# Pair 0's low halves between the unpackings of the weight words, its first products tile by tile, and five small operations moved from VectorE to GpSimd

## The chip, the cores and the metric

The kernel runs on one core of a Trainium2 chip. The metric is the device time of one execution in microseconds. Five engines work at the same time, each on its own queue of instructions in a fixed order: TensorE (PE; its weight loads are shown apart as PEld), VectorE (DVE), ScalarE (ACT), GpSimd (POOL), and SyncE (SP), which only issues transfers here. An instruction that must wait for another engine holds up everything behind it on its own queue.

## The reference, cut to what matters

```python
W  = cond_weights[condition]                    # (64, 64, 64): one of 16 matrices for each batch
h  = einsum('bct,bcd->bdt', x, W)               # x: (64, 64, 1024) f32
p  = qweight.reshape(N, groups, 3)              # words that hold 6-bit fields
v0, v1, v2, v3 = p[..,0] & 63, p[..,0] >> 6 & 63, p[..,1] & 63, p[..,2] & 63
w  = (unpacked - zero_point) * scale            # (1024, 1024)
out = x + einsum('bsk,nk->bsn', h, w) + bias
```

So there are two products in a row. The first mixes the 64 channels of a batch by a matrix that the batch's condition selects; the second multiplies each of the 64 x 64 rows by a 1024 x 1024 weight matrix that has to be unpacked from words.

## The kernel before, in words

**Tiling.** The 64 batches go as 32 pairs; a pair fills the 128 partitions with 2 x 64 channels. For each pair, stage 1 makes `ph`, the first product, turned so that the features of the sequence lie on the partitions in 8 tiles of 128 (`kt` 0 to 7). It is split into two float16 halves: `hh`, the rounded value (ScalarE), and `hl`, the rest (VectorE). Stage 2 multiplies both by the unpacked words `q16`, read as float16 numbers, and sums 8 tiles x 2 halves x 2 banks of 512 columns into `po`: 32 matmuls of 512 columns a pair. The zero point, scale, bias and residual come after it, in `zero_points`, `scale_out`, `accumulate` and their early forms.

**Order.** The schedule is by hand (`manual_schedule`): each engine executes its instructions in the order in which the Python code calls the helpers. From pair 3 on, `window(p)` repeats one pattern; pairs 0 to 2 have an opening written out call by call (lines 573 to 713), and the whole change lies there.

**The opening.** Pairs 0 and 1 (group 0) use a float32 first product on the raw selected matrices, since the split table isn't there yet: `early_stage1` (L436), `early_high` (L444, ScalarE, one pass for each half of 64 columns), `early_low` (L451, VectorE, likewise one pass for each half). Pair 0's `ph` lies in two tiles, `ph0a` for `kt` 0 to 3 and `ph0b` for 4 to 7. `unpack` (L153 and L155, VectorE) turns the words into `q16`: tiles 0 and 1 singly as their words land, then 2-3, 4-5 and 6-7. `stage2_tiles` (L520) issues the products of some tiles of a pair; with `[0]` the `hh` part alone, with `[1]` the `hl` part. `weights_turn` puts a 128-column matmul `pt` (L174) into TensorE's queue, the first step towards the powers of two that scale the 16 matrices.

**The table of matrices.** `weights_scaled` (GpSimd, L196) scales them, `weights_high` (ScalarE, L201) and `weights_low` (VectorE, L204) split them into the table `tab`. `select_pair` (L249) then copies two entries of `tab` for each pair; for pairs 2 to 7 GpSimd does it, 12 copies, with one large product, `zsc`, after the first two. The numbers of the entries are loaded into GpSimd's registers by `conditions_of` (L235), early in its queue. Stage 1 of pair 2 needs the first two copies. Behind the copies GpSimd makes the low half of pair 2's and 3's sums (`sums_low`, L354), which the matmuls `pu` of `feature_sums` (L365) read.

**Group 1 (pairs 2 and 3)** is split on the whole: `magnitudes` (L273, ScalarE) sums the absolute values, `bounds` (L277, a matmul `pl`) adds them over the partitions, `scales` (L138, L139, L142, VectorE) makes powers of two, `stacked_high` (L322, ScalarE) and `stacked_low` (L330, VectorE, both inputs in SBUF) write the halves of x into `xa`. `FIRST` is pair 2, `SECOND` pair 3.

**The end of pairs 0 and 1.** `early_zero_points` (L464, ScalarE), `early_minus` (L469) and `early_res` (L475, both VectorE); `early_minus` needs the factor `u` that `early_unscales` (L432, two operations of 64 partitions x 1 element a pair) makes. `weights_hot` (L208) makes a one-hot table of the conditions that `weights_of_batches` (L224) needs much later.

Of the kernel before, what the change touches and what calls it, by code (L numbers as in the profile page):

```python
# [14 lines left out]
ALU = mybir.AluOpType  # L15
# [4 lines left out]
QUNIT = 2.0**-24  # L20
# [9 lines left out]
def adaln_ffn(ctx: ExitStack, tc: tile.TileContext, x, cond, cw, qw, ws, wz, bias, out):  # L30
    nc = tc.nc
    B, C, T = x.shape
    _, _, NK, _ = cw.shape
# [6 lines left out]
    LO, HI = slice(0, C), slice(C, P)  # L40
# [10 lines left out]
    unpacking = ExitStack()  # L51
# [31 lines left out]
    cb = const.tile([NK, B], I32, name="cb")  # L83
# [44 lines left out]
    kio = const.tile([NK, 1], F32, name="kio")  # L128
# [6 lines left out]
    def powers(sums, up, down, least=True):  # L135

        if least:
            nc.vector.tensor_scalar(sums, sums, LEAST, None, ALU.max)  # L138
        nc.vector.tensor_scalar(  # L139
            down.bitcast(I32), sums.bitcast(I32), EXPONENT, EXPONENT, ALU.bitwise_and, ALU.bitwise_xor  # L140
        )
        nc.vector.tensor_scalar(up.bitcast(I32), sums.bitcast(I32), EXPONENT, None, ALU.bitwise_and)  # L142
# [5 lines left out]
    def unpack(kt, n=1):  # L148

        w = kt if kt < 2 else kt - 2 if kt < 6 else kt - 4  # L150
        to, of_ = q16[:, kt : kt + n, :], qr[:, w : w + n, :]
        if kt in (2, 3, 6, 7):
            nc.vector.tensor_scalar(to, of_, 6 if kt < 4 else 8, 63, ALU.logical_shift_right, ALU.bitwise_and)  # L153
        else:
            nc.vector.tensor_scalar(to, of_, 63, None, ALU.bitwise_and)  # L155
# [9 lines left out]
    hot = const.tile([P, B], BF, name="hot")  # L165
# [23 lines left out]
    def weights_powers():  # L189

        powers(tmp["pw"], tmp["pw"], wdn)
# [8 lines left out]
    def weights_high():  # L200
        nc.scalar.copy(tab[:, :, 0, :], wsc)  # L201
# [3 lines left out]

    def weights_hot():

        nc.vector.tensor_scalar(hot[0:NK, :], cb, kio[:, 0:1], None, ALU.is_equal)  # L208

    def weights_own():  # L210

# [44 lines left out]
    st = {}  # L256
    BOTH = slice(0, 2)

    def magnitudes(g, i):
        if g not in st:  # L260
            st[g] = {
                "l1": sp.tile([P, 2], BF, name="l1"),
                "u": sp.tile([P, 2], F32, name="u"),
                "hs": sp.tile([P, 2], F32, name="hs"),
                "xs": sp.tile([P, 2], F32, name="xs"),
                "up": sp.tile([P, 2], F32, name="up"),
                "down": sp.tile([P, 2], F32, name="down"),
                "hf": ap.tile([P, 2, T], F16, name="hf"),
                "lf": ap.tile([P, 2, T], F16, name="lf"),
                "xa": ap.tile([P, 2, 2, T], F16, name="xa"),  # L270
            }
        junk = ap.tile([P, T], BF, name="junk", bufs=1)
        nc.scalar.activation(junk, xts[g][:, i, :], AF.Abs, accum_out=st[g]["l1"][:, i : i + 1])  # L273

    def bounds(g, sl=BOTH):
        pl = ps_s.tile([P, 2], F32, name="pl", tag="s")
        nc.tensor.matmul(pl[:, sl], lhsT=ones, rhs=st[g]["l1"][:, sl], start=True, stop=True)  # L277
        st[g]["pl"] = pl

    def scales(g, sl=BOTH):  # L280
        powers(st[g]["pl"][:, sl], st[g]["up"][:, sl], st[g]["down"][:, sl])
# [23 lines left out]
    def split_2(g, i, ts_=ALL):  # L305

        nc.vector.scalar_tensor_tensor(  # L307
            st[g]["lf"][:, i, ts_],
            xts[g][:, i, ts_],
            st[g]["down"][:, i : i + 1],  # L310
            st[g]["hf"][:, i, ts_],
            ALU.mult,
            ALU.subtract,
        )
# [11 lines left out]
    def stacked_low(g, i, j):  # L326

        h, o = HALVES_OF[j]
        xa = st[g]["xa"]
        nc.vector.scalar_tensor_tensor(  # L330
            xa[o, i, j], xts[g][h, i], st[g]["down"][h, i : i + 1], xa[h, i, j], ALU.mult, ALU.subtract
        )
# [7 lines left out]
    def stack_low(g, sl=BOTH, ts_=ALL):  # L340
        lf, xa = st[g]["lf"], st[g]["xa"]
        nc.sync.dma_start(xa[HI, sl, 0, ts_], lf[LO, sl, ts_])
        nc.sync.dma_start(xa[LO, sl, 1, ts_], lf[HI, sl, ts_])
# [41 lines left out]
    updown = const.tile([P, 2, 2, 2], F32, name="updown")  # L385

    def early_select(p, j, eng):

        h = (LO, HI)[j]
        k = eng.value_load(cb[0:1, 2 * p + j : 2 * p + j + 1], min_val=0, max_val=NK - 1)  # L390
        for n, o in enumerate((LO, HI)):
            to = wbd[h, p, j * D + n * D // 2 : j * D + (n + 1) * D // 2]
            of_ = wq[o, ds(k, 1), :].rearrange("p o d -> p (o d)")
            if eng is nc.scalar:
                eng.copy(to, of_)
            else:
                eng.tensor_copy(to, of_)

    def early_weights(p):

        wl = const.tile([P, 1], F32, name=f"wl{p}")
        nc.vector.tensor_reduce(wl, wbd[:, p, :], AX.X, ALU.max, apply_absolute_value=True)
        nc.vector.tensor_scalar(wm[:, p, :], half, wl[:, 0:1], None, ALU.mult)
# [23 lines left out]
    def early_scales(p):  # L427
        powers(tmp["pl"], updown[:, p, 0, :], updown[:, p, 1, :], least=False)

    def early_unscales(p):  # L430
        for j, h in enumerate((LO, HI)):
            nc.vector.tensor_scalar(st[0]["u"][h, p : p + 1], updown[h, p, 0, j : j + 1], 0.5 / QUNIT, None, ALU.mult)  # L432

    def early_stage1(p, ph, kts=range(KT)):
        for kt in kts:
            nc.tensor.matmul(  # L436
                ph[:, kt % ph.shape[1], :, :], lhsT=xts[0][:, p, ts(kt, P)], rhs=wbd[:, p, :], start=True, stop=True
            )
# [6 lines left out]
                hs_pair[p][0][:, kts, h], ph[:, :, j, :], AF.Copy, scale=updown[:, p, 1, j : j + 1]  # L445
            )

    def early_low(p, ph, kts):
        hh, hl = hs_pair[p]
        for j, h in enumerate((LO, HI)):  # L450
            nc.vector.scalar_tensor_tensor(  # L451
                hl[:, kts, h], ph[:, :, j, :], updown[:, p, 1, j : j + 1], hh[:, kts, h], ALU.mult, ALU.subtract
            )
# [19 lines left out]
    def early_res(p):  # L473
        tmp["res", p] = late.tile([P, N], F32, name=f"res{p}")
        nc.vector.tensor_tensor(tmp["res", p], pos[p], scb, ALU.mult)  # L475
# [34 lines left out]
    def stage1_low(p, ph, kts=slice(0, KT)):  # L510
        hh, hl = hs_pair[p]
        nc.vector.tensor_tensor(hl[:, kts, :], ph[:, kts, :], hh[:, kts, :], ALU.subtract)  # L512
# [17 lines left out]
    def stage2_tiles(p, kts, ks=range(2)):  # L530
        if p not in pos:
            pos[p] = ps_o[1 + p % 2].tile([P, N], F32, name="po", tag="po")
        products(pos[p], p, kts, ks, BANKS, BANKS)
# [40 lines left out]
    FIRST, SECOND = slice(0, 1), slice(1, 2)  # L574
    LOWER, UPPER = slice(0, KT // 2), slice(KT // 2, KT)
# [7 lines left out]
    ph0a, ph0b = [ps_e.tile([P, KT // 2, 2, D], F32, name="ph0") for _ in range(2)]  # L583
# [2 lines left out]
    early_select(0, 1, nc.scalar)  # L586
    early_select(1, 0, nc.gpsimd)
    early_select(1, 1, nc.gpsimd)
    for n in range(2, 8):
        conditions_of(n, nc.gpsimd)  # L590
    weights_largest()
# [8 lines left out]
    early_stage1(0, ph0b, range(4, KT))  # L600
    early_bounds(0, 3)
    early_scales(0)
    early_weights(1)
    early_high(0, ph0a, LOWER)
    early_high(0, ph0b, UPPER)
    early_stage1(1, ph1)
    unpack(0)
    unpack(1)
    early_low(0, ph0a, LOWER)
    early_magnitudes(1, 0, ALL, nc.scalar)  # L610
    stage2_tiles(0, range(0, 2), [0])
    unpack(2, 2)
    early_low(0, ph0b, UPPER)
    early_rows(1, 0)
    weights_turn()
    weights_diagonal()
    weights_hot()
    unpack(4, 2)
    stage2_tiles(0, range(0, 2), [1])
    unpack(6, 2)  # L620
    early_sums(0)
    early_sums(1)
# [1 line left out]
    weights_bounds()  # L624
    early_bounds(1, 1)
    early_scales(1)
    weights_powers()
    weights_scaled()
    weights_own()
# [8 lines left out]
    stacked_high(1, 0)  # L638
    for j in range(2):
        stacked_low(1, 0, j)  # L640
    weights_high()
    stage2_tiles(0, range(6, KT))
    early_feature_sums(0)
    early_feature_sums(1)
    magnitudes(1, 1)
    early_zero_points(0)
    early_unscales(0)
    weights_up()
    weights_low()
    unpacking.close()  # L650
    late = ctx.enter_context(tc.tile_pool(name="late", bufs=1))
    select_pair(2, nc.gpsimd)
    nc.gpsimd.tensor_tensor(zsc, zsb, scb, ALU.mult)
    for n in range(3, 8):
        select_pair(n, nc.gpsimd)


    stage2_tiles(1, range(0, 4), [0])
    stage2_tiles(1, range(0, 4), [1])
    bounds(1, SECOND)  # L660
    scales(1, SECOND)
    early_minus(0)
    early_res(0)
    stage2_tiles(1, range(4, 7))
    stacked_high(1, 1)
    stacked_low(1, 1, 0)
    ph = stage1(2)
    stage1_high(2, ph, LOWER)
    stage1_high(2, ph, UPPER)
# [2 lines left out]
    magnitudes(2, 0)  # L672
    magnitudes(2, 1)
    stage1_low(2, ph)
    stacked_low(1, 1, 1)
    weights_of_batches()
    unscales(1)
    early_unscales(1)


    sums_high(1)
# [4 lines left out]
    ph = stage1(3)  # L686
# [7 lines left out]
    split_1(2, 0)  # L694
    stack_high(2, FIRST)
    split_2(2, 0)
    stack_low(2, FIRST)
    split_1(2, 1)
    stack_high(2, SECOND)
    stage1_low(3, ph)  # L700
    stage2_bank(2, 0, [1])
    stage2_bank(2, 1, [1])
    split_2(2, 1)
# [81 lines left out]
    p = NP - 1  # L785
# [81 lines left out]
```

## Time and profile before

| what | value |
| --- | --- |
| time, median of 3 runs | 266.2 us (266.08 to 266.25) |
| the profiled execution: its own time | 266.35 us |
| the profiled execution: span of its instructions | 264.6 us |
| TensorE busy | 260.1 us, 98% of the span |
| VectorE busy | 202.1 us, 76% |
| ScalarE busy | 162.0 us, 61% |
| GpSimd busy | 175.8 us, 66% |
| granted TensorE clock, mean | 0.999 |

The time of an execution holds 1.75 us more than the span, which begins with the first instruction of the program and ends with its last. Lines of the profile that list instructions give the start in us from the start of the span, the duration in us, the engine, the line of the code, the operation, the tile written and the tiles read (`out<-in`), the shapes, how many instructions are merged, and in brackets how long the engine sat idle before it and what ended that. A merged line hides a long instruction among short ones, so short windows are asked for where single instructions matter. A record of an instruction ends a little after the next one on its engine may start.

### The profile page before, as it was taken

What the parts mean: (1) busy time and instruction counts of PE and PEld (TensorE: products, weight loads), DVE (VectorE), ACT (ScalarE), POOL (GpSimd) and SP (SyncE); (2) the same over time, 40 slices, a digit from 0 to 9 for tenths busy, and PEclk for the clock granted to TensorE, in tenths of its full rate; (3) what the DMA queues carried; (4) which work ended last, traced back from release to release, by engine and by line L of the source; (5) the groups of instructions that cost most, each with busy time, mean ns of one, the idle gap of its engine ahead of it and who ended that gap; (6) DMA issues with size and microseconds to landing.
All of it is one profiled execution on the core that took longest, in us unless ns stands there. A gap on an engine that the chain in (4) does not pass through costs nothing.

```text
span 264.6 us, 5769 instructions
## 1 busy us (share of the span) xinstructions
PE 260.1 (98%) x2175; PEld 140.2 (53%) x2175; DVE 202.1 (76%) x272; ACT 162.0 (61%) x290; POOL 175.8 (66%) x106
## 2 busy tenths in 40 slices
PE   8999999999999999999999999999999999999995
PEld 8645555555455555455555445555545555545544
DVE  4889999695967949498695968949497695955535
ACT  4899899655766556686555667556586555634100
POOL 5037367879595996959689595986929286495200
PEclk9999999999999999999999999999999999999999
DMA  6993087759639786579867797676976664551104
GB/s 207 388 408 153 5 190 245 215 177 290 192 103 310 212 286 171 186 229 242 258 185 226 245 260 243 155 246 209 288 221 188 199 180 144 165 161 79 81 7 154
DMA packets 32300, 53.60 MB, mean 203 GB/s; under 512 B 15120, under 2 KB 15504, under 8 KB 32272
## 3 DMA queue, kind: packets, MB, share of 16 engines
q1 hardware_dynamic: 32240, 53.23, 65.0%
q8 instruction: 17, 0.28, 0.4%
q14 instruction: 11, 0.09, 0.1%
q10 hardware_dynamic: 32, 0.00, 0.0%
HBM read 20.19 MB, written 16.78 MB: 140 GB/s over the span
## 4 chain that ended last, share of the span: by engine, by line
PE 95%; DMA 2%; SPq 1%; DVE 1%; issue 0%
PE po L520 81%; PE ph L496 11%; PE pe L520 3%; DMA qr<-in_L_ffn_qweight_dram 2%; SPq L66 1%; PE pu L365 1%; DVE hl L451 0%; SPq L78 0%; SPq L89 0%; DVE pe L561 0%; PE pu L458 0%; DVE xt L566 0%; PE pl L277 0%; DVE q L155 0%; PE pb__635 L224 0%
## 5 line engine op out<-in xcount | busy, mean ns | idle before, releaser
L520 PE MATMUL po<-q,hh 128*128 128x512 f16 x496 | 118.4, 379 | 0.1
L520 PE MATMUL po<-q,hl 128*128 128x512 f16 x496 | 118.3, 379 | 0.1
L556 POOL TENSOR_TENSOR xt<-xt,zt 128x1024 f32<-128x1024 f32 x28 | 78.9, 2838 | 48.3 <-ACT zt L554 48.3
L520 PEld LDWEIGHTS <-hl 128*128 128x128 f16 x528 | 51.4, 98 | 59.8 <-DVE hl L451 0.5
L508 ACT CAST hh<-ph 128x1024 f16<-128x1024 f32 (+1 forms) x31 | 30.4, 983 | 79.2 <-PE ph L496 41.5
L520 PEld LDWEIGHTS <-hh 128*128 128x128 f16 x528 | 49.3, 98 | 52.1 <-issue 0.3
L549 POOL TENSOR_TENSOR xt<-xt,bib 128x1024 f32<-128x1024 f32 x32 | 74.6, 2354 | 2.1 <-issue 2.1
L561 DVE SCALAR_TENSOR_TENSOR po<-po,u,scb 128x1024 f32<-128x1024 f32 x27 | 34.7, 1287 | 49.2 <-PE po L520 49.2
L307 DVE SCALAR_TENSOR_TENSOR lf<-xt,down,hf 128x1024 f16<-128x1024 f32 x28 | 60.1, 2185 | 0.0
L512 DVE TENSOR_TENSOR hl<-ph,hh 128x1024 f16<-128x1024 f32 x30 | 36.5, 1216 | 0.1
L496 PEld LDWEIGHTS <-xa 128*128 128x128 f16 x960 | 32.1, 98 | 7.1
L566 DVE TENSOR_TENSOR xt<-po,xt 128x1024 f32<-128x1024 f32 x27 | 33.1, 1225 | 1.9
L496 PE MATMUL ph<-wst,xa 128*128 128x64 f16 x960 | 32.9, 193 | 0.0
L273 ACT ACTIVATE junk<-xt 128x1024 bf16<-128x1024 f32 x30 | 31.7, 1056 | 0.8
L297 ACT ACTIVATE hf<-xt,down 128x1024 f16<-128x1024 f32 x28 | 31.9, 1143 | 0.1
L554 ACT ACTIVATE zt<-zsc,hs 128x1024 f32<-128x1024 f32 x28 | 30.5, 1136 | 0.0
L358 ACT ACTIVATE xh<-xh,xs 64x1 f16<-64x1 f16 x52 | 12.4, 287 | 0.5
L485 POOL TENSOR_TENSOR xt<-xt,res 128x1024 f32<-128x1024 f32 x4 | 9.4, 2361 | 0.0
L249 POOL COPY wst<-tab 128x128 f16 x12 | 4.9, 454 | 5.1 <-DVE tab L204 5.1
L196 POOL TENSOR_TENSOR wsc<-w,wdn 128x512 f32<-128x512 f32 x2 | 2.1, 1045 | 8.0 <-DVE pw L142 8.0
L520 PE MATMUL pe<-q,hh 128*128 128x128 f16 (+2 forms) x32 | 6.7, 272 | 0.0
L520 PE MATMUL pe<-q,hl 128*128 128x128 f16 (+2 forms) x32 | 6.6, 272 | 0.0
(90 smaller groups left out, 121.9 us busy)
## 6 DMA issues: line engine op xcount, KB each, us to landing
out_dram<-xt SPq DMA_DIRECT2D x31, 512.0 KB, 3.0
xt<-in_x_dram SPq DMA_DIRECT2D x14, 1024.0 KB, 7.0
xa<-hf SPq DMA_DIRECT2D x24, 256.0 KB, 4.0
xa<-lf SPq DMA_DIRECT2D x24, 256.0 KB, 3.8
wst<-tab SPq DMA_DIRECT2D x48, 32.0 KB, 3.0
xt<-in_x_dram SPq DMA_DIRECT2D x4, 256.0 KB, 4.4
xt<-in_x_dram SPq DMA_DIRECT2D x2, 512.0 KB, 8.1
xa<-hf SPq DMA_DIRECT2D x8, 128.0 KB, 2.4
```

The costliest lines, as they stand in the source:

```text
L273: nc.scalar.activation(junk, xts[g][:, i, :], AF.Abs, accum_out=st[g]["l1"][:, i : i + 1])
L297: nc.scalar.activation(st[g]["hf"][:, i, ts_], xts[g][:, i, ts_], AF.Copy, scale=st[g]["down"][:, i : i + 1], accum_out=st[g]["xs"][:, i : ...
L307: nc.vector.scalar_tensor_tensor(st[g]["lf"][:, i, ts_], xts[g][:, i, ts_], st[g]["down"][:, i : i + 1], st[g]["hf"][:, i, ts_], ALU.mult, ...
L496: nc.tensor.matmul(ph[:, kt, j, :], lhsT=st[g]["xa"][:, i, j, ts(kt, P)], rhs=wsts[g][:, i, a, j, :], start=(a == 0), stop=(a == 1),)
L508: nc.scalar.copy(hs_pair[p][0][:, kts, :], ph[:, kts, :])
L512: nc.vector.tensor_tensor(hl[:, kts, :], ph[:, kts, :], hh[:, kts, :], ALU.subtract)
L520: nc.tensor.matmul(po[:, a], lhsT=hs_pair[p][k][:, kt, :], rhs=qT[:, kt, c], start=(kt == 0 and k == 0), stop=(kt == KT - 1 and k == 1),)
L549: nc.gpsimd.tensor_tensor(xt, xt, bib, ALU.add)
L554: nc.scalar.activation(zt, zsc, AF.Copy, scale=st[g]["hs"][:, i : i + 1])
L556: nc.gpsimd.tensor_tensor(xt, xt, zt, ALU.subtract)
L561: nc.vector.scalar_tensor_tensor(po, po, st[g]["u"][:, i : i + 1], scb[:, cols], ALU.mult, ALU.mult)
L566: nc.vector.tensor_tensor(xts[g][:, i, cols], po, xts[g][:, i, cols], ALU.add)
```

## The change

Seven things change, all in the opening. Nothing that is computed changes.

1. `early_low` of `ph0a` is issued half by half: the first half ahead of `unpack(0)`, the second between `unpack(0)` and `unpack(1)`. Before, both stood behind `unpack(1)`.
2. TensorE does pair 0's tiles 0 and 1 tile by tile, `hh` and `hl` of tile 0 and then of tile 1, instead of `hh` of both, then `pt`, then `hl` of both. `pt` comes behind all eight matmuls.
3. `weights_hot` moves from VectorE, where it stood ahead of `unpack(4, 2)`, to GpSimd, ahead of the register loads of `conditions_of`.
4. `early_unscales` of both pairs moves from VectorE to GpSimd, behind those loads and ahead of `weights_scaled`.
5. On ScalarE `magnitudes(1, 1)` (pair 3's) goes ahead of `weights_high`.
6. `bounds(1, SECOND)` goes one tile earlier in TensorE's queue, and on VectorE `scales(1, SECOND)` goes ahead of `weights_up` and `weights_low`.
7. On VectorE both `stacked_low` of pair 3 stand together, ahead of `stage1_low(2)`; before, the second stood behind it.

The other moved lines of the diff (`unpacking.close`, `late`, the calls of `select_pair`, `stage1_low(3, ph)`) leave each engine's own order as it was.

```diff
     def weights_hot():
 
-        nc.vector.tensor_scalar(hot[0:NK, :], cb, kio[:, 0:1], None, ALU.is_equal)
+        nc.gpsimd.tensor_scalar(hot[0:NK, :], cb, kio[:, 0:1], None, ALU.is_equal)
 
     def early_unscales(p):
         for j, h in enumerate((LO, HI)):
-            nc.vector.tensor_scalar(st[0]["u"][h, p : p + 1], updown[h, p, 0, j : j + 1], 0.5 / QUNIT, None, ALU.mult)
+            nc.gpsimd.tensor_scalar(st[0]["u"][h, p : p + 1], updown[h, p, 0, j : j + 1], 0.5 / QUNIT, None, ALU.mult)
 
-    def early_low(p, ph, kts):
+    def early_low(p, ph, kts, js=range(2)):
         hh, hl = hs_pair[p]
-        for j, h in enumerate((LO, HI)):
+        for j in js:
+            h = (LO, HI)[j]
...
     early_select(1, 0, nc.gpsimd)
     early_select(1, 1, nc.gpsimd)
+    weights_hot()
     for n in range(2, 8):
         conditions_of(n, nc.gpsimd)
...
     early_scales(0)
+    early_unscales(0)
     early_weights(1)
     early_high(0, ph0a, LOWER)
     early_high(0, ph0b, UPPER)
     early_stage1(1, ph1)
+    early_low(0, ph0a, LOWER, [0])
     unpack(0)
+    early_low(0, ph0a, LOWER, [1])
     unpack(1)
-    early_low(0, ph0a, LOWER)
     early_magnitudes(1, 0, ALL, nc.scalar)
-    stage2_tiles(0, range(0, 2), [0])
+    stage2_tiles(0, range(0, 2))
     unpack(2, 2)
     early_low(0, ph0b, UPPER)
     early_rows(1, 0)
     weights_turn()
     weights_diagonal()
-    weights_hot()
     unpack(4, 2)
-    stage2_tiles(0, range(0, 2), [1])
     unpack(6, 2)
...
     early_bounds(1, 1)
     early_scales(1)
+    early_unscales(1)
     weights_powers()
     weights_scaled()
...
     for j in range(2):
         stacked_low(1, 0, j)
+    magnitudes(1, 1)
     weights_high()
     stage2_tiles(0, range(6, KT))
     early_feature_sums(0)
     early_feature_sums(1)
-    magnitudes(1, 1)
     early_zero_points(0)
-    early_unscales(0)
+    unpacking.close()
+    late = ctx.enter_context(tc.tile_pool(name="late", bufs=1))
+    stage2_tiles(1, range(0, 4), [0])
+    stage2_tiles(1, range(0, 3), [1])
+    bounds(1, SECOND)
+    scales(1, SECOND)
     weights_up()
     weights_low()
-    unpacking.close()
-    late = ctx.enter_context(tc.tile_pool(name="late", bufs=1))
     select_pair(2, nc.gpsimd)
     nc.gpsimd.tensor_tensor(zsc, zsb, scb, ALU.mult)
     for n in range(3, 8):
         select_pair(n, nc.gpsimd)
-    stage2_tiles(1, range(0, 4), [0])
-    stage2_tiles(1, range(0, 4), [1])
-    bounds(1, SECOND)
-    scales(1, SECOND)
     early_minus(0)
     early_res(0)
+    stage2_tiles(1, [3], [1])
     stage2_tiles(1, range(4, 7))
     stacked_high(1, 1)
-    stacked_low(1, 1, 0)
+    for j in range(2):
+        stacked_low(1, 1, j)
     ph = stage1(2)
...
     stage1_low(2, ph)
-    stacked_low(1, 1, 1)
     weights_of_batches()
     unscales(1)
-    early_unscales(1)
...
     split_2(2, 0)
+    stage1_low(3, ph)
     stack_low(2, FIRST)
     split_1(2, 1)
     stack_high(2, SECOND)
-    stage1_low(3, ph)
```

## The prediction

> **What bounds the kernel now.** I read first the chain that ended last, in order of time, then the instructions of VectorE, ScalarE and TensorE up to 13 us, then what waits in the opening up to 38 us.
>
> ```profile
> PE 95%; DMA 2%; SPq 1%; DVE 1%; issue 0%
> ```
>
> ```profile
> 3.55 5.52 DMA qr<-in_L_ffn_qweight_dram
> ...
> 9.43 0.88 DVE hl L451 x2
> 10.31 0.05 issue
> 10.36 2.76 PE po L520 x12
> ...
> 29.36 0.21 PE pu L365 x4
> ...
> 36.56 0.97 PE ph L496 x32
> ```
>
> TensorE is the end of everything from 10.36 us on. From 38 us the chain is one row of matmuls, two pairs in 15.8 us, so a change counts only by how much earlier TensorE is there. Ahead of 10.36 the chain is the landing of the words and VectorE's low halves.
>
> ```profile
> 7.72 0.23 DVE L403 TENSOR_SCALAR wm<-half,wl 128x2 f32<-128x2 f32 x1
> 8.44 0.43 DVE L155 TENSOR_SCALAR q<-qr 128x1024 uint16<-128x1024 uint16 x1 [0.49 <-DMA qr<-in_L_ffn_qweight_dram]
> 9.09 0.43 DVE L155 TENSOR_SCALAR q<-qr 128x1024 uint16<-128x1024 uint16 x1 [0.22 <-DMA qr<-in_L_ffn_qweight_dram]
> 9.43 0.87 DVE L451 SCALAR_TENSOR_TENSOR hl<-ph,updown,hh 128x256 f16<-128x256 f32 x2
> 10.22 0.68 DVE L153 TENSOR_SCALAR q<-qr 128x2048 uint16<-128x2048 uint16 x1
> ```
>
> ```profile
> 7.46 1.57 ACT L444 ACTIVATE hh<-ph,updown 128x256 f16<-128x256 f32 x4 [0.95 <-DVE updown L139]
> ```
>
> ```profile
> 8.92 1.24 PE L520 MATMUL po<-q,hh 128*128 128x512 f16 x4
> 10.00 0.22 PE L174 MATMUL pt<-eye,wmx 128*128 128x128 bf16 x1
> 10.36 1.04 PE L520 MATMUL po<-q,hl 128*128 128x512 f16 x4
> ...
> 12.99 0.16 PE L424 MATMUL pl<-pb,all_ones 128*128 128x2 bf16 x1
> 13.08 0.59 PE L520 MATMUL po<-q,hh 128*128 128x512 f16 x2
> ```
>
> The reader is to see VectorE idle for 0.49 us before the first unpacking and 0.22 before the second, while `hh` is partly ready, and TensorE's holes: 9.35 to 9.57, 10.05 to 10.36, and some 0.07 before 13.08 (the unpacking of tiles 4-5, 12.35 + 0.67, ends at 13.02).
>
> **The change, part by part. The head (parts 1 and 2).** ScalarE's four passes start 0.37 us apart and last 0.47, so the first ends at 7.93, the second at 8.30. VectorE is free at 7.95. One L451 lasts 0.48, and its successor starts 0.39 after it (9.43, 10.22): the first half runs from 7.98 and the unpacking at 8.44 isn't moved, since the words land then. An unpacking's successor starts after 0.34 (9.09, 9.43): second half 8.78 to 9.26, second unpacking 9.17 to 9.60 (its words landed at 9.07), third 9.52 to 10.20. A dependent matmul starts 0.05 after its producer's end (10.31, 10.36), and a 512-column matmul takes 0.216. TensorE: `hh` of tile 0 at 8.92, `hl` at 9.35 (ready 9.31), `hh` of tile 1 at 9.78 (ready 9.65), `hl` at 10.21, `pt` at 10.64; `pt` now lies on the path with a quarter of 0.216. Tile 2 starts at 10.70 instead of 11.23. Tile 4 comes 1.72 + 0.06 later, at 12.49 (its unpacking is long done, see part 3): 0.58 earlier than 13.08. Bounds of the gain: 0.18 if the first half starts only when the words land and moves all behind it by 0.4, 0.63 with no cost for `pt`. I take 0.58, since the rows show the place free.
>
> **Part 3.** `hot` left VectorE's queue: 0.16 us there (12.19 to 12.35). With the idle 0.22 and the first half's 0.39 gone too, tiles 4-5 are unpacked at 12.2. On GpSimd it delays register loads that nobody needs before 21 us, and `hot` itself is read at 24.78. Cost 0.
>
> **Part 4.** VectorE loses four L432 rows, 0.31 us before 19.87 and 0.42 between 28.55 and 28.97. GpSimd gets five small operations. The profile doesn't show these there; the nearest rows are its copies of 64x32 (0.20) and its `xh` rows (0.19 to 0.29), so 1.0 to 1.5 us, and no less than nothing. I take 1.0.
>
> ```profile
> L235 POOLq TENSOR_LOAD <-cb x12: 282/284/297, 5.9 to 12.6; - x12
> ```
>
> The loads end at about 13.15, and `wsc` starts at 14.21 now, waiting for VectorE, which will be ready 0.7 sooner. So `wsc` stays near 14.2 and ends near 16.3; ScalarE takes it up at 18.4 (below). Slack 2 us: cost 0.
>
> **Part 5.** ScalarE is in one piece from 8.90 to 13.61, so `hh` of pair 1 gains only 0.1 (needed at 16.3, there at 14.9). `scales(1, FIRST)` follows TensorE, 0.58 earlier; L322 starts at 14.9 instead of 15.43, the magnitudes at 17.4, the table's high half at 18.4 to 19.4, `zt` till 20.5. All hidden under matmuls; only past 20.1 would a later high half move L204 with it. SyncE's queue keeps its order, and no transfer is added or moved.
>
> **Part 6 adds a wait, and this is where I expect most of the gain to go.**
>
> ```profile
> 20.04 1.22 DVE L204 TENSOR_TENSOR tab<-wsc,tab 128x1024 f16<-128x1024 f32 x1
> 21.18 0.16 DVE L138 TENSOR_SCALAR pl<-pl 128x1 f32<-128x1 f32 x1
> ...
> 24.09 1.40 DVE L330 SCALAR_TENSOR_TENSOR xa<-xt,down,xa 64x1024 f16<-64x1024 f32 x1
> 25.51 1.23 DVE L512 TENSOR_TENSOR hl<-ph,hh 128x1024 f16<-128x1024 f32 x1
> ```
>
> `weights_low` (L204) now stands behind L138, which waits for `pl`. `pl` stands behind the third `hl` tile of pair 1: 19.93 in today's times, 19.35 after. L138 follows by 0.24 (14.80 to 15.04), the next free slot by 0.34, `up_w` takes 0.17: L204 starts at 20.10, not earlier than today's 20.04. VectorE, ready at 18.9, sits idle for 0.6 us before it. GpSimd's copies hang on L204:
>
> ```profile
> 21.32 0.52 POOL L249 COPY wst<-tab 128x128 f16 x2 [5.07 <-DVE tab L204]
> 21.81 2.36 POOL L653 TENSOR_TENSOR zsc<-zsb,scb 128x1024 f32<-128x1024 f32 x1
> 24.12 4.40 POOL L249 COPY wst<-tab 128x128 f16 x10
> 28.82 0.46 POOL L354 TENSOR_TENSOR xh<-xs,xh 64x2 f16<-64x2 f32 x2 [0.30 <-ACT xh L348]
> ```
>
> ```profile
> 24.35 1.29 POOL L249 COPY wst<-tab 128x128 f16 x1
> ```
>
> ```profile
> 29.33 0.24 PE L365 MATMUL pu<-xh,wst 128*128 128x2 f16 x4
> ```
>
> Today GpSimd has 0.30 us to spare before `xh`, and `pu` already waits 0.11 for `xh` (`pl` at 29.19, `pu` 0.03 behind it elsewhere). The copies take 0.24 each, except two of 1.29 and 1.28 that began under an L330 and ended just after it: an operation of VectorE with two inputs in SBUF and one of GpSimd don't run together. From 53.3 us on the same is seen between L307 and L556 (L307 1.28 us alone, up to 3.38 under an L556).
>
> One rule of the skill speaks against the change here. The Trainium skill, Advanced Engine Details and Errata, section VectorE Performance Modes, says that VectorE's second SBUF port is shared with GpSimd, so that GpSimd's instructions and VectorE's two-port modes block each other. By it each of the five moved operations could hold up an unpacking; at 0.2 us each and with 0.6 idle on VectorE behind them the sum would stay what it is.
>
> **Part 7 with it.** VectorE after L204: L469 at 21.24, L475 at 22.56, the first L330 at 23.82. But `zsc` runs 0.06 later, till 24.23, so the L330 really begins near 24.03 and ends at 25.3; one copy slips in, the second L330 holds the next one till 26.8, and eight more copies end at 28.70 (today 28.52). `xh` follows at 28.66 and 28.86, ends at 29.06, `pu` at 29.11. Both ends: 29.0 if the copies are held as today, 29.25 if the `xh` need 0.27 each. TensorE could have been there at 29.22 - 0.58 = 28.64. It is 0.22 earlier than today: 0.36 of 0.58 is given back.
>
> Stage 1 of pair 3 needs L512 done, which has moved behind both L330: 26.7 to 27.9, so it starts near 27.95 instead of 28.26, hidden by the later wait for `pu`.
>
> **Behind it.** VectorE is 0.54 earlier from L469 of pair 1 on (0.12, and 0.42 of part 4). So `hl` of pair 3 is ready at 34.1, TensorE there at 34.4: today's hole of 0.05 before 34.66 closes; so do the 0.04 in pair 4's first product (0.97 against 0.93 in the chain), which waits for a transfer issued 0.5 earlier. Sum: 0.58 - 0.36 + 0.09 = 0.31. Profiled execution 266.35 - 0.31 = 266.04; it stands 0.15 above the median of 266.2, so **265.9 us**.
>
> **The rivals.**
> - **GpSimd keeps up.** If the two L330 standing together, one partly under `zsc`, hold up the copies once instead of twice, GpSimd has 1 us more, and the wait for L512 (27.75 at best, 0.51 gained) is what remains: 0.51 + 0.09 = 0.60, 265.6. For it: one copy less may fall under an L330. Against: in the rows every L330 over the copies cost one of them 1.0.
> - **The head doesn't do what it says.** If the first half starts 0.4 late (ScalarE still reads the same `ph0a`), the unpackings go 0.4 later, 0.18 is left at tile 4, L204 goes to 20.5 and `pu` to 29.5: 0.2 lost, 0.09 won, 266.3. Against: the same operation took 0.48 in all four rows.
> - **Slower: the five operations delay the table.** `wsc` must be done by 18.4, so they may occupy GpSimd from 13.15 to 16.3, 0.63 us each. Beyond, each 0.1 us per operation moves the table's halves, the copies and `pu` by 0.5. At 0.8 each the 0.31 are gone and 0.55 lost: 266.75; at 0.9 267.2. Against: no small operation of GpSimd takes over 0.3 unheld.
>
> **How the numbers follow.** Faster or slower by 0.2% (0.53 us) is about what a measurement of this kernel can tell from no change. Forecast 0.56 (265.75 to 266.05 by its bounds, within 0.2%), GpSimd keeps up 0.22 (faster), head fails 0.08 (same), slower 0.08; 0.06 for what I don't see, 0.02 of it faster, 0.04 slower. Faster 0.24, same 0.64, slower 0.12. The range takes in the first three: 265.5 to 266.4.
>
> **What would show it.** Right: TensorE without a hole from 8.92 to 12.5, tile 4 at 12.5; VectorE idle 0.6 before L138 near 19.6; L204 near 20.1; `xh` with no idle before it; a hole of some 0.4 before `pu` near 29.1. Wrong: `unpack(0)` later than 8.5; `pu` following `pl` at once; `wsc` later than 16; copies of GpSimd held three times or once.

## The result: 0.2% slower, and the profile after

The changed kernel takes 266.85 us (median of 15 runs, 266.12 to 267.56), the kernel before 266.34 (15 runs, 265.76 to 266.80). The ratio is 1.0022, with a 95% interval of 1.0013 to 1.0031, so 0.35 to 0.83 us slower. Forecast was 0.3 us faster, with a range up to 266.4: wrong in sign. The profiled execution has a span of 265.4 us (before 264.6).

In the chain that ended last TensorE isn't the end of everything from 10.36 us on any more. It runs through the table and GpSimd's copies to the sums (start, duration, what):

```profile
8.13 0.33 issue
8.46 0.47 ACT hh L444
8.96 0.48 DVE hl L452
9.44 0.28 DVE q L155
...
22.40 0.11 POOL wst L249
...
29.76 0.20 POOL xh L354
29.95 0.07 issue
30.03 0.20 POOL xh L354
30.27 0.24 PE pu L365 x4
30.51 6.93 PE po L521 x32
```

Two things are to be seen there. First, the opening hangs on ScalarE's pass (L444) and the first low half (L452 now) instead of the landing of the words. VectorE's instructions around it:

```profile
8.35 0.23 DVE L403 TENSOR_SCALAR wm<-half,wl 128x2 f32<-128x2 f32 x1
8.96 0.48 DVE L452 SCALAR_TENSOR_TENSOR hl<-ph,updown,hh 128x256 f16<-128x256 f32 x1 [0.38 <-ACT hh L444]
9.36 0.42 DVE L155 TENSOR_SCALAR q<-qr 128x1024 uint16<-128x1024 uint16 x1
9.69 0.47 DVE L452 SCALAR_TENSOR_TENSOR hl<-ph,updown,hh 128x256 f16<-128x256 f32 x1
10.09 0.42 DVE L155 TENSOR_SCALAR q<-qr 128x1024 uint16<-128x1024 uint16 x1
```

```profile
8.09 1.57 ACT L444 ACTIVATE hh<-ph,updown 128x256 f16<-128x256 f32 x4 [1.19 <-DVE updown L139]
```

ScalarE's four passes began at 8.09 and were 0.36 apart, so the first ended at 8.56 and the second at 8.93. The low half of the first pass could have begun near 8.58, when VectorE was free; it began at 8.96, and the wait in brackets is for ScalarE. Second, the middle of the opening, on VectorE, GpSimd and TensorE:

```profile
20.48 0.17 DVE L138 TENSOR_SCALAR pl<-pl 128x1 f32<-128x1 f32 x1 [0.63 <-PE pl L277]
...
21.09 1.22 DVE L204 TENSOR_TENSOR tab<-wsc,tab 128x1024 f16<-128x1024 f32 x1
...
24.80 2.82 DVE L330 SCALAR_TENSOR_TENSOR xa<-xt,down,xa 64x1024 f16<-64x1024 f32 x2
27.65 1.22 DVE L513 TENSOR_TENSOR hl<-ph,hh 128x1024 f16<-128x1024 f32 x1
```

```profile
22.37 0.52 POOL L249 COPY wst<-tab 128x128 f16 x2 [5.68 <-DVE tab L204]
22.86 2.37 POOL L661 TENSOR_TENSOR zsc<-zsb,scb 128x1024 f32<-128x1024 f32 x1
25.17 4.51 POOL L249 COPY wst<-tab 128x128 f16 x10
29.76 0.47 POOL L354 TENSOR_TENSOR xh<-xs,xh 64x2 f16<-64x2 f32 x2
```

```profile
28.93 1.11 PE L497 MATMUL ph<-wst,xa 128*128 128x64 f16 x32 [0.20 <-DVE hl L513]
29.88 0.17 PE L277 MATMUL pl<-l,ones 128*128 128x2 bf16 x1
30.27 0.24 PE L365 MATMUL pu<-xh,wst 128*128 128x2 f16 x4 [0.23 <-POOL xh L354]
```

VectorE idles for 0.63 us before L138 (forecast 0.6), the table's low half (L204) comes late, GpSimd has no slack before `xh`, and TensorE has two holes: 0.36 us ahead of pair 3's first product, where before had none, and 0.36 between `pl` and `pu`, where before had 0.11.

The position of the whole opening differs too, and not by the change: the first instruction that differs is `hot` on GpSimd, at 6.37 us. TensorE's forty warming matmuls took 4.12 us in the profile before and 4.45 after; the third line is from the run e1 below.

```profile
1.06 4.12 PE L579 MATMUL pc<-dummy 128*128 128x128 bf16 x40 [1.06 <-DVE one L110]
```

```profile
1.06 4.45 PE L580 MATMUL pc<-dummy 128*128 128x128 bf16 x40 [1.06 <-DVE one L110]
```

```profile
1.06 3.68 PE L580 MATMUL pc<-dummy 128*128 128x128 bf16 x40 [1.06 <-DVE one L110]
```

The starts of these matmuls lie 0.107 us apart at first and 0.056 later. The switch came at 4.74 us before, at 3.80 in e1, and not within the forty (after 5.2 us) in the changed kernel's profile. The Trainium skill, TensorE: Matmul & The Clock Gate, section What's actually happening, tells of a gate that halves TensorE's clock until a window of activity that runs on its own has passed, so that the moment varies from run to run; a spacing that halves, at a moment that differs from run to run, agrees with it, but the spread here, from 3.80 to over 5.2 us, is wider than the 500 ns either way that it states. So a start in one profile can't be set beside the same start in another. Below I count from the start of tile 4 (the seventeenth 512-column matmul), behind which TensorE sets the pace of the rest. In the changed kernel's profile it is this one:

```profile
13.39 0.59 PE L521 MATMUL po<-q,hh 128*128 128x512 f16 x2
```

### The profile page after: what moved, and what is told of

It is laid out like the page before. It is cut to its first block, busy times and chain, and to the rows that moved or that the text cites. A ratio compares the mean times of both kernels' runs of the same rounds, so it can differ in the third digit from the quotient of the medians.

```text
span 265.4 us, 5769 instructions
## 1 busy us (share of the span) xinstructions
PE 260.6 (98%) x2175; PEld 140.7 (53%) x2175; DVE 199.3 (75%) x267; ACT 161.9 (61%) x290; POOL 177.0 (67%) x111
## 4 chain that ended last, share of the span: by engine, by line
PE 90%; issue 3%; POOL 3%; DVE 2%; ACT 0%; POOLq 0%
PE po L521 74%; PE ph L497 10%; PE pe L521 3%; POOL wst L249 2%; PE pc L580 2%; PE ph L436 1%; POOL wsc L196 1%; PE pu L365 1%; DVE q L155 0%; DVE hl L452 0%; DVE q L153 0%; ACT hh L444 0%; POOLq L249 0%; POOL xh L354 0%; DVE pe L562 0%
## 5 line engine op out<-in xcount | busy, mean ns | idle before, releaser
L307 DVE SCALAR_TENSOR_TENSOR lf<-xt,down,hf 128x1024 f16<-128x1024 f32 x28 | 58.0, 2108 | 0.0
L348 ACT CAST xh<-xs 64x2 f16<-64x2 f32 x30 | 5.8, 192 | 0.4
```

The lines of the kernel that those rows point to most:

```text
L307: nc.vector.scalar_tensor_tensor(st[g]["lf"][:, i, ts_], xts[g][:, i, ts_], st[g]["down"][:, i : i + 1], st[g]["hf"][:, i, ts_], ALU.mult, ...
```

## The experiments

Three theories at first. A: the head is exposed to a late first product. B: part 6 (the table behind the bound of pair 3) costs more than the head gains. C: the changed kernel's runs only had late openings. The readings from all profiles, in us: *a* is the start of ScalarE's first pass (L444), *b* the start of tile 4, then the start of the table's low half (L204), of `pu` (L365) and of the last matmul of the last pair's stage 1, each less *b*. The ratio is to the kernel before, in the same series.

| run | ratio (95%) | a | b | b - a | table - b | pu - b | last - b |
| --- | --- | --- | --- | --- | --- | --- | --- |
| before | | 7.46 | 13.08 | 5.62 | 6.96 | 16.25 | 234.21 |
| changed | 1.0022 (1.0013, 1.0031) | 8.09 | 13.39 | 5.30 | 7.70 | 16.88 | 234.75 |
| e4 changed, again | 1.0027 (1.0016, 1.0037) | 8.18 | 13.48 | 5.30 | 7.70 | 16.88 | 234.74 |
| e1 head alone | 1.0002 (0.9992, 1.0012) | 6.99 | 12.29 | 5.30 | 6.97 | 16.25 | 234.21 |
| e2 part 6 alone | 1.0024 (1.0015, 1.0033) | 8.27 | 13.28 | 5.01 | 7.84 | 16.93 | 235.01 |
| e3 changed less part 6 | 1.0000 (0.9990, 1.0010) | 7.67 | 12.97 | 5.30 | 6.99 | 16.26 | 234.13 |
| e5 before, late | 1.0012 (1.0002, 1.0021) | 7.89 | 13.00 | 5.11 | 6.96 | 16.26 | 234.21 |
| e6 head alone, late | 1.0018 (1.0006, 1.0030) | 8.43 | 13.73 | 5.30 | 6.97 | 16.26 | 234.22 |
| e7 words first | 1.0002 (0.9992, 1.0012) | 7.21 | 12.83 | 5.62 | 7.00 | 16.27 | 234.13 |
| e8 parts 3, 4, 5, 7 | 0.9997 (0.9988, 1.0005) | 7.94 | 12.95 | 5.01 | 7.00 | 16.28 | 234.15 |
| e9 product late | 1.0051 (1.0031, 1.0071) | 7.43 | 12.73 | 5.30 | 7.70 | 16.30 | 235.16 |
| e10 as e8, 32 warming | 0.9997 (0.9984, 1.0011) | 7.98 | 12.99 | 5.01 | 6.99 | 16.26 | 234.13 |
| e11 as e7, 32 warming | 0.9987 (0.9976, 0.9999) | 7.24 | 12.70 | 5.46 | 6.99 | 16.27 | 234.13 |
| e12 as e3, 32 warming | 1.0000 (0.9982, 1.0018) | 7.63 | 12.94 | 5.31 | 6.99 | 16.26 | 234.13 |
| e13 table first | 1.0011 (1.0000, 1.0023) | 7.25 | 12.85 | 5.60 | 6.99 | 16.26 | 234.13 |
| e14 words first alone | 0.9994 (0.9985, 1.0003) | 7.76 | 12.78 | 5.02 | 7.00 | 16.27 | 234.27 |

### The head and part 6 apart

**e1, the head alone on the kernel before:**

```diff
-    unpack(0)
-    unpack(1)
-    early_low(0, ph0a, LOWER)
+    early_low(0, ph0a, LOWER, [0])
+    unpack(0)
+    early_low(0, ph0a, LOWER, [1])
+    unpack(1)
...
-    stage2_tiles(0, range(0, 2), [0])
+    stage2_tiles(0, range(0, 2))
...
-    stage2_tiles(0, range(0, 2), [1])
```

> The kernel before with parts 1 and 2 of the change alone (low halves between the unpackings, TensorE tile by tile). Theory A (the head is exposed: the first low half waits for both of ScalarE's passes over ph0a, so the first unpacking no longer starts when the words land): tile 2 starts 0.2 to 0.3 us earlier than before where the first product of pair 0 is early, and later than before where it is late; the time is between -0.3 and +0.3 us of before, 0 on average. Theory B (the head is worth its 0.3, and part 6 takes it): -0.3 to -0.45 us. Theory C (the changed kernel was slower by the chance of late openings alone): -0.3 us or more.

**e2, part 6 alone on the kernel before:**

```diff
-    weights_up()
-    weights_low()
...
+    stage2_tiles(1, range(0, 4), [0])
+    stage2_tiles(1, range(0, 3), [1])
+    bounds(1, SECOND)
+    scales(1, SECOND)
+    weights_up()
+    weights_low()
     select_pair(2, nc.gpsimd)
...
-    stage2_tiles(1, range(0, 4), [0])
-    stage2_tiles(1, range(0, 4), [1])
-    bounds(1, SECOND)
-    scales(1, SECOND)
+    stage2_tiles(1, [3], [1])
```

> The kernel before with part 6 alone (the bound of pair 3 one tile earlier, its scales ahead of the low half of the table). Theory B: the low half of the table starts at about 20.7 us instead of 20.04, GpSimd's copies end near 29.2 instead of 28.5, pu starts near 29.7 instead of 29.3: +0.3 to +0.4 us. Theories A and C: no more than 0.1 us.

**e3, the changed kernel with that edit undone** (the low half of the table ahead of the bound again, the bound behind all four tiles).

> The changed kernel with part 6 undone, all other parts kept. Theory B: the low half of the table starts before 20 us (counted with an opening as early as before's), pu no longer waits for GpSimd: 0.35 to 0.5 us faster than the changed kernel, so equal to before or up to 0.2 us faster. Theory A: within 0.15 us of the changed kernel, so 0.35 us or more slower than before. Theory C: no slower than before.

**e4, the changed kernel once more.**

> The changed kernel once more, for a second profile and the same chip as the others. Theories A and B: 0.3 to 0.7 us slower than before, with GpSimd's copies ending 0.4 us or more later than before even when pair 0's first product is as early as before's; A alone has that first product late and unpack(0) behind ScalarE. Theory C: no slower than before when the opening is early.

Measured: 266.42, 267.19, 266.34 and 267.25 us, against 266.37 for before. Part 6 alone makes a kernel as slow as the changed one, and without it the changed kernel is as fast as before. Theory B stands, at nearly twice the expected size, and C falls. A isn't what slows the kernel, but what it says of the head, nothing on average, holds as far as e1 can tell: its interval reaches 0.27 us either way. In e2 VectorE waits for the bound ahead of the table, as it does in the changed kernel, though a bit less:

```profile
20.51 0.17 DVE L138 TENSOR_SCALAR pl<-pl 128x1 f32<-128x1 f32 x1 [0.42 <-PE pl L277]
...
21.12 1.22 DVE L204 TENSOR_TENSOR tab<-wsc,tab 128x1024 f16<-128x1024 f32 x1
```

TensorE pays in several places, two of which the next lines show: pair 3's first product stops after two matmuls for the second L330, and `pu` comes 0.28 after `pl`.

```profile
28.64 0.22 PE L496 MATMUL ph<-wst,xa 128*128 128x64 f16 x2
29.04 1.05 PE L496 MATMUL ph<-wst,xa 128*128 128x64 f16 x30 [0.18 <-DVE xa L330]
29.93 0.17 PE L277 MATMUL pl<-l,ones 128*128 128x2 bf16 x1
30.21 0.24 PE L365 MATMUL pu<-xh,wst 128*128 128x2 f16 x4
```

TensorE's holes behind tile 4, from its matmul starts, are 0.20 us in before, 0.72 in the changed kernel and 0.98 in e2; the last column of the table, 0.54 and 0.80 above before's, says the same. With the other parts but without part 6 (e3) only the 0.12 ahead of `pu` is left, where before has 0.11: 234.13, 0.08 below before.

### What in part 6 costs

**e9, the changed kernel with GpSimd relieved:** its large product moves from ahead of the ten copies to behind the low halves of the sums.

```diff
     select_pair(2, nc.gpsimd)
-    nc.gpsimd.tensor_tensor(zsc, zsb, scb, ALU.mult)
...
     sums_low(1, nc.gpsimd)
+    nc.gpsimd.tensor_tensor(zsc, zsb, scb, ALU.mult)
```

> The changed kernel with GpSimd's large product (2.36 us) moved from ahead of the last ten copies to behind the low halves of the sums, so that GpSimd has 2 us to spare there. If part 6 costs through GpSimd's chain (table, product, copies, sums, pu): pu follows the bound of pair 4 and 5 within 0.15 us, the copies end before 28 us, and the kernel is 0.3 to 0.6 us faster than the changed kernel. If it costs through VectorE alone (stage 1 of pair 3 waiting for the low half of pair 2): that hole of 0.36 us stays and the kernel is less than 0.15 us faster than the changed kernel.

Measured 267.54 us (six runs, the profiled one the fastest of them), ratio 1.0051: slower still, against every theory. Up to `pu` the expectation holds: `pu` follows `pl` by 0.03 us, the copies end at 25.59, the hole ahead of pair 3's first product shrinks from 0.36 to 0.14, and `pu` is back at tile 4 + 16.30 (before 16.25, changed 16.88). But the product then held VectorE:

```profile
30.18 1.20 DVE L284 SCALAR_TENSOR_TENSOR u<-up,wupb 128x2 f32<-128x2 f32 x1
```

```profile
29.01 2.35 POOL L684 TENSOR_TENSOR zsc<-zsb,scb 128x1024 f32<-128x1024 f32 x1
```

```profile
32.93 1.89 PE L521 MATMUL po<-q,hh 128*128 128x512 f16 x8 [0.19 <-DVE res L476]
35.26 0.60 PE L521 MATMUL po<-q,hl 128*128 128x512 f16 x2 [0.44 <-DVE hl L513]
```

An operation of two elements a partition, which took 0.16 us a little earlier (at 28.33), took 1.20, and ended at 31.38, as the product did at 31.36. Everything behind it on VectorE was late, and TensorE got holes of 0.35 and 0.61 us by matmul starts. So up to `pu` it is GpSimd's chain that part 6 lengthens, and this was no place for the product.

**e13, VectorE's order alone undone:**

```diff
+    weights_up()
+    weights_low()
     bounds(1, SECOND)
     scales(1, SECOND)
-    weights_up()
-    weights_low()
```

> The changed kernel with one pair of calls exchanged on VectorE alone: the low half of the table goes ahead of pair 3's scales again; TensorE keeps the changed order, with the bound one tile earlier. If part 6 costs by VectorE's wait ahead of the table: the low half of the table starts 7.0 us behind tile 4 instead of 7.7, pu waits no more than 0.15 us, 0.35 to 0.55 us faster than the changed kernel, so within 0.1 us of before. If it costs by TensorE's own new order: no faster than the changed kernel.

```profile
19.84 1.22 DVE L204 TENSOR_TENSOR tab<-wsc,tab 128x1024 f16<-128x1024 f32 x1 [0.26 <-ACT tab L201]
20.98 0.16 DVE L138 TENSOR_SCALAR pl<-pl 128x1 f32<-128x1 f32 x1
```

```profile
28.04 1.10 PE L497 MATMUL ph<-wst,xa 128*128 128x64 f16 x32
28.97 0.17 PE L277 MATMUL pl<-l,ones 128*128 128x2 bf16 x1
29.11 0.24 PE L365 MATMUL pu<-xh,wst 128*128 128x2 f16 x4
```

With TensorE's order as changed and only two calls exchanged, the table is back at tile 4 + 6.99, and TensorE's only hole behind tile 4 is the one ahead of `pu` that before has too. In the profile it is VectorE's wait ahead of the table that costs, not TensorE's order. The time, 266.62 us, gives a ratio of 1.0011, against 1.0022 and 1.0027 of the changed kernel: 0.3 to 0.4 us better, at the lower end of what was expected, but still 0.3 above before, where 0.1 at most was expected; the interval (1.0000 to 1.0023) reaches down to before. The profile behind tile 4 is the same as e3's, so what is over lies in the head, in chance or in executions unlike the profiled one. The runs fall in two groups, five of 265.77 to 266.07 us and seven of 266.61 to 267.06, and the profile is of the first; what made the second stays open.

### What the head does

**e5 and e6, a late first product:** before and e1 with `WARM = 52` instead of 40, twelve warming matmuls more.

> The kernel before with 52 warming matmuls instead of 40, so that pair 0's first product comes some 0.7 to 1.2 us later; for comparison with the same edit on the head-only kernel. Theory A (before's head waits for the landing of the words and has slack to a late first product): tile 4 comes no more than 0.2 to 0.5 us later than in the slow-starting profiles of before's head (13.3 us), 5.0 us behind the start of ScalarE's first pass; the time is 0.1 to 0.5 us longer than before. Without such slack (theory of the prediction, both heads follow the same product) it is 0.7 to 1.2 us longer.

> The kernel before with parts 1 and 2 of the change and 52 warming matmuls. Theory A: tile 4 comes 5.3 us behind the start of ScalarE's first pass, so about 0.3 us later than in the late kernel with before's head; the time is 0.2 to 0.4 us longer than that kernel's. The prediction's theory (the head gains in any case): 0.3 to 0.5 us shorter than that kernel's.

Both took 266.78 us; by their ratios the head's kernel is 0.16 us slower (0.0006 of 266.3), within the intervals, so the times don't show what A expected. The profiles do. In all eight profiles with the changed kernel's head the first low half starts 0.03 to 0.04 us after the **second** of ScalarE's passes ends, and tile 4 follows the first pass by 5.30 us in six of them and 5.31 in a seventh; in e13, the eighth, by 5.60, since the first unpacking had to wait another 0.21 us for its words there (8.81). The instructions in the trace say the same: the first of two passes raises no semaphore, the second does, and the first half waits for that one. Why the program was built so, no run here shows. With before's head tile 4 came at 12.95 to 13.28 whether the first pass started at 7.46 or at 8.27. So the new head gains if the pass starts ahead of about 7.7 to 7.8 (13.0 to 13.1 less 5.30) and loses behind it. In the ten profiles with forty warming matmuls the pass starts at 7.65 on average, about where neither happens.

**e7, a head that keeps the first unpacking on the words,** on e3:

```diff
-    early_low(0, ph0a, LOWER, [0])
     unpack(0)
-    early_low(0, ph0a, LOWER, [1])
+    early_low(0, ph0a, LOWER)
     unpack(1)
```

> The changed kernel with part 6 undone and both low halves between the two unpackings, so that the first unpacking again waits for its words alone. Theory A: tile 2 starts near 11.05 us when the first product is early, near 11.5 when it is late, so never later than with before's head; the time is 0.1 to 0.4 us shorter than before (265.95 to 266.25 where before has 266.35). If the head gains nothing for another reason: equal to before within 0.1.

**e8, parts 3, 4, 5 and 7 alone** (e3 with before's head).

> Parts 3, 4, 5 and 7 of the change alone, without the head and without part 6. Theory B (part 6 is all that makes the changed kernel slower): 0 to 0.15 us shorter than before, by the holes ahead of tile 4 and ahead of the sums' matmuls. If one of these parts had a cost of its own: longer than before by 0.1 us or more.

Measured 266.28 and 266.18, before 266.28. Tile 2 of e7 came at 11.05 and tile 4 at 12.83, as expected, but the time didn't follow: a miss for A. Parts 3, 4, 5 and 7 cost nothing that shows (e8, interval 0.9988 to 1.0005).

### Less warming

The first half of pair 0 had landed when ScalarE began its sum at 4.31 to 4.77 us in four of the profiles, while forty warming matmuls lasted till 5.5 in two of them. So `WARM = 32` on e8 (**e10**), on e7 (**e11**) and on e3 (**e12**), and **e14**: before with e7's head and 32, without the other parts.

> Parts 3, 4, 5 and 7 with 32 warming matmuls instead of 40. Where TensorE's clock rises late, the 40 last until 5.3 us though pair 0's first half has landed at 4.3 to 4.8; with 32 they end by 4.5. Before's head waits for the words, so tile 4 stays near 13.0 us, and the time within 0.15 us of the same kernel with 40 (0.1 us under before); slower by 0.3 or more if the clock rises later for want of work.

> The changed kernel without part 6, the low halves both behind the first unpacking, with 32 warming matmuls. Tile 4 at 12.8 to 12.9 us nearly always: 0.1 to 0.3 us faster than before, 0.05 to 0.2 faster than the kernel with before's head and 32.

> The changed kernel without part 6, its own head, with 32 warming matmuls. Theory A: the head follows pair 0's first product, 5.3 us from the start of ScalarE's first pass to tile 4, so with the product early it gains: tile 4 at 12.3 to 12.8 us and a time 0.2 to 0.5 us under before. If the head gained nothing for another reason: equal to before's head with 32.

> The kernel before with nothing but the head that keeps the first unpacking on the words (both low halves between the two unpackings, TensorE tile by tile) and 32 warming matmuls. If the head makes the gain of the faster version: 0.25 to 0.45 us faster than before. If the operations moved to GpSimd and part 7 are needed for it: tile 4 0.2 us earlier than before, but less than 0.15 us faster at the end, with new holes behind tile 4.

Measured: 266.19, 265.87 and 266.14 us against 266.29, and e14 266.09 against 266.18. Only e11 is faster than before by more than its interval, and barely: ratio 0.9987 (0.9976 to 0.9999), some 0.35 us. As one of fourteen ratios it may be chance. Its head, as VectorE and TensorE show it:

```profile
8.29 0.43 DVE L155 TENSOR_SCALAR q<-qr 128x1024 uint16<-128x1024 uint16 x1 [0.56 <-DMA qr<-in_L_ffn_qweight_dram]
8.63 0.87 DVE L452 SCALAR_TENSOR_TENSOR hl<-ph,updown,hh 128x256 f16<-128x256 f32 x2
9.42 0.42 DVE L155 TENSOR_SCALAR q<-qr 128x1024 uint16<-128x1024 uint16 x1
```

```profile
8.77 0.59 PE L521 MATMUL po<-q,hh 128*128 128x512 f16 x2
9.56 0.60 PE L521 MATMUL po<-q,hl 128*128 128x512 f16 x2 [0.20 <-DVE hl L452]
```

The first unpacking waits for the words again, not for ScalarE. e12, from which A expected 0.2 to 0.5 us, gave nothing clear; in its profile TensorE's clock rose late and the first pass started at 7.63, so the head had little to gain. e14 is between its two alternatives: tile 4 at 12.78, but 0.14 us more behind it than e7 (234.27 against 234.13), which parts 3, 4, 5 and 7 together save, and 0.16 us of gain by its ratio, not clear of chance.

## Why the prediction was wrong, point by point

**The head (parts 1 and 2), 0.58 us: wrong.** The step that failed is "the first half runs from 7.98 and the unpacking at 8.44 isn't moved". I took the first half to need the first of ScalarE's passes; in all eight profiles with this head it waited for the second. With before's opening it would have begun at 8.33, and tile 4 would have come at 7.46 + 5.30 = 12.76, 0.32 earlier. That is not the whole mistake. I took one profiled opening for the rule, while the first pass starts anywhere from 6.99 to 8.27 us with forty warming matmuls. Before's head has the landing words as cover for a late product; the new one has none. On average the head is worth nothing, to within 0.27 us (e1: 1.0002). The rival "the head doesn't do what it says" had the right place and size, a first half 0.4 late (8.96 against 8.56), at 0.08.

**Part 6: the right mechanism, under-sized.** VectorE's idle time (0.63 against "0.6"), L204 behind the bound (tile 4 + 7.70, forecast 20.10 - 12.49 = 7.61), the copies (8.59 from L204 to the last copy's end, forecast 8.60) and the two copies held, by 1.00 and 1.09, came as written. The term "`xh` follows at 28.66 and 28.86, ends at 29.06, `pu` at 29.11" was mis-sized: 0.41 from the last copy's end to `pu`, measured 0.59, since the first `xh` began 0.08 after the end of the last copy instead of ahead of it, and the second 0.27 after the first instead of 0.20 (before's own two are 0.27 apart, 28.82 and 29.09). Another 0.09 is in L204: `up_w` started 0.44 after L138 (20.48 to 20.92), where the sum had "the next free slot by 0.34". Up to `pu` it makes 0.63 (16.88 less 16.25) instead of 0.37 (29.11 - 12.49 - 16.25). "Behind it", 0.09 of before's holes closed, was right. So from tile 4 on the change costs 0.54, where the sum had 0.28.

**Together:** 0.58 of gain that isn't there and 0.26 of cost too little make 0.84; the forecast of -0.31 becomes +0.53, and +0.51 was measured. Since e1 leaves 0.27 us either way, so close an agreement is partly luck.

**Parts 3, 4, 5 and 7: right, cost 0** (e8: 0.9997). GpSimd's five operations took 1.56 us, a little over the bound of 1.5, with the table's source at 14.64 instead of 14.2, and nobody waited:

```profile
13.46 1.10 POOL L432 TENSOR_SCALAR u<-updown 64x1 f32<-64x1 f32 x4 [6.62 <-DVE q L155]
14.64 2.05 POOL L196 TENSOR_TENSOR wsc<-w,wdn 128x512 f32<-128x512 f32 x2
```

The hold between VectorE and GpSimd that the prediction weighed against these operations shows, but it is GpSimd that waits. In the profiles of the changed kernel and of e4 the first of the four small operations began during the last unpacking. It took 0.30 and 0.40 us, where it took 0.22 in the other runs that have it, and ended 0.08 us behind the unpacking, which took its 0.69 either way:

```profile
12.99 0.69 DVE L153 TENSOR_SCALAR q<-qr 128x2048 uint16<-128x2048 uint16 x1
13.46 0.30 POOL L432 TENSOR_SCALAR u<-updown 64x1 f32<-64x1 f32 x1 [6.62 <-DVE q L155]
```

So the slower rival by these operations fell, and the kernel became slower by a step that the forecast had and sized too small. The rival "GpSimd keeps up" fell too: the copies were held twice.

## What to carry to other kernels

An instruction that is pulled forward into an idle slot takes on that slot's cover: ask what the slot was waiting for, and whether the pulled instruction's own input is as punctual in every execution, not in the one that was profiled. A wait put ahead of the first link of a long chain on another engine (here 0.6 us ahead of the table, 9 us ahead of the matmul that pays) costs as soon as that chain's slack, 0.30 us here, is used up: counted from tile 4 the table came 0.74 us later and `pu` 0.63. Count such chains from a fixed point behind the opening, and compare profiles by those distances.

## What the runs showed of the hardware that I had not expected

- TensorE's half-speed start ended anywhere from 3.78 us (e9) to 5.5 (e6, with fifty-two warming matmuls) in these profiles, in which the first matmul started at 1.06. With forty warming matmuls pair 0's first product began between 4.58 and 5.30, and ScalarE's first pass, with landings that vary too, between 6.99 and 8.27.
- The hold between VectorE and GpSimd is not only for large operations: a VectorE operation of two elements a partition with both inputs in SBUF went from 0.16 to 1.20 us under GpSimd's product (e9).
- Small operations of 64 partitions x 1 element took 0.20 to 0.22 us on GpSimd when nothing held them, 0.14 to 0.15 on VectorE.
